# Moving the loads of the output weights in a cross-attention kernel, and dealing the first batch's projection steps anew

## The chip, the core and the metric

The kernel runs on one core of a Trainium2 chip. The metric is device time in microseconds (us), lower is better. The kernel before took 574.34 us, the median of three runs (573.46, 574.34, 575.16). One execution was also profiled; it took 574.06 us, of which 572.2 us are the span between its first and last instruction. All durations below come from that execution, and its times count from the start of the span.

## What is computed

Cross-attention with a layer norm in front and a residual behind, in float32:

```
x   = layernorm(hidden) * gamma + beta          # hidden: 8 x 256 x 1024
Q   = split_heads(x @ Wq.T)                     # 32 heads of 32
K,V = split_heads(ctx), split_heads(ctx)        # ctx: 8 x 256 x 1024
p   = softmax(where(mask, Q K^T / sqrt(32), -inf))
out = hidden + merge_heads(p V) @ Wout.T
```

## The kernel before

The order of instructions is written out by hand: the program calls the engines in the order in which they run, and every engine, SP's DMA queue among them, takes its instructions in that order. A wait of the first in a queue holds all behind it.

**Slots.** The work is cut into 64 slots, one for each of the 8 batches and 8 groups of 4 heads. A loop over n (near line 920) issues slot n as a pipeline. TensorE (PE) makes the scores of group n+1 (`scores`, L479), then the values of group n-2 (`values`, L622), and then whatever matmuls the slot has besides: projections of queries (`make_q`, L340, for the first three batches, `query_product`, L440, later) and steps of the output projection (`product_steps`, L708). VectorE (DVE) and ScalarE (ACT) do the softmax of group n+1 (L515, L519, L526), GpSimd (POOL) multiplies by the reciprocal sums (L528), DVE transposes in 32 x 32 blocks (L534), and ACT sets half of the result aside (L540).

**The copies within the chip.** The transposed probabilities pT have to change partitions before `values` can use them. The tail of each softmax (L595) issues on SP: two copies pT<-pT (L600), then the loads that the slot wants (a list named `between`: keys L136 or values L144, x L130, the residual rows r L150, and in the first eight slots one load of output weights, `load_wo`, L173), and then two copies pT<-pc (L604). The latter overwrite what the former have read, so they wait until those have landed. In slots 0 to 6 the tail is held back and issued in the softmax of the next slot. After it may come pieces of the normalised x on their way to another layout (`move_x`, L327).

**The output projection** of a batch runs during the slots of the next one. It is computed as seven products of half-size blocks (a Strassen-like scheme), each of four steps, so 28 steps for a batch. A step is one 128 x 128 by 128 x 512 product, which the trace shows as two matmuls. The products in their order are A11, A12, S2, S3, A22, S1, S4. Their weights are four blocks of the output weights as loaded (B11, B21, B12, B22; each comes as two loads of 512 KB, `pair` 0 and 1) and four sums of them that POOL forms in the slots 3 to 14 (`sum_wo`, L183: T3 = B22 - B12, T2 = T3 + B11, T4 = B21 - T2, and T1 = B12 - B11 in B12's place).

`steps_of` (L660) says how many of the 28 steps go to which slot of the next batch, and to which of three places in it: 0 is ahead of the slot's values, 1 right behind them, 2 at the slot's end. A plan entry (0, 6, 0) is thus six steps at place 1. For the first batch (b = 0) its own plan holds. Its product A11 goes to a PSUM bank of its own, which ACT copies to SBUF as P1 (`keep_p1`, L716). A12 goes to the one bank of the pool `ps_o`. In slot 10 DVE adds that bank and the residual rows r(0,0) (`store`, L750), after POOL has added P1 to r(0,0) (`add_p1`, L741), and SP sends the sum out. S2 then begins in the same bank, so its first step waits for that store. The next bank reads are `take` (L746) in slots 11 and 12.

**The head**, ahead of the loop, loads the first x, the query weights wq (eight loads of 512 KB, L167), two pairs of keys, one of values and the second x. The weights need no other buffer than their own, so a load of wo waits for no reader. SP has a limited set of DMA semaphores, used in turn, so a DMA also waits for the one that last used its semaphore, some eight DMAs earlier.

**"Traffic of B11"** in the name of the change is the copy of B11's *query* weights to memory and back (`keep_wq`, L400, and `load_ring`, L407). The change leaves it as it is.

Of the kernel before, what the change touches and what calls it, by code (L numbers as in the profile page):

```python
# [59 lines left out]
def xattn_kernel(  # L60
# [16 lines left out]
    NQ = NC  # L77
# [85 lines left out]
    B11, B21, B22, T1, T2, T3, T4 = range(7)  # L163
    B12 = T1

    def load_wq(o):
        nc.sync.dma_start(wq[:, o], wq_[o])  # L167

    def load_wo(which, pair):

        k, h = {B11: (0, 0), B21: (1, 0), B12: (0, 1), B22: (1, 1)}[which]
        rows = woT[ds((NK * k + 2 * pair) * P, 2 * P), ts(h, 512)]
        nc.sync.dma_start(  # L173
            wo[:, which, ts(pair, 2)], rows.rearrange("(c p) q -> p c q", c=2)
        )
# [31 lines left out]
    load_v(0)  # L207
    for o in range(5, 8):
        load_wq(o)


    xnTs, mvs, rstds = {}, {}, {}
# [416 lines left out]
    def copy_at(n):  # L629
# [4 lines left out]
        for r, pv in enumerate(pvs.pop(n)):  # L634
# [20 lines left out]
    STEPS = ((0, 0, 0), (4, 0, 3), (0, 1, 2), (0, 2, 2), (0, 2, 1), (0, 1, 2), (0, 0, 3), (0, 1, 2),  # L655
             (0, 2, 0))
# [3 lines left out]
    def steps_of(b):  # L660
        if b == B - 2:
            return ENDS
        if b == 0:
            return STEPS[:1] + ((0, 6, 0), (0, 2, 2)) + STEPS[3:]
        return STEPS[:1] + ((0, 7, 0),) + STEPS[2:] if b in P1_ASIDE else STEPS

    assert all(sum(map(sum, steps_of(b))) == len(PRODUCTS) * NK for b in range(B - 1))

    def operand(b, name):
# [228 lines left out]
    for b in range(B - 1):  # L898
        done, ends = 0, b == B - 2
        for i, counts in enumerate(steps_of(b)):  # L900
            n = NQ * (b + 1) + i
            for place, k in enumerate(counts):
                steps.setdefault((n, place), []).append((b, range(done, done + k)))
                done += k
        for i, *what in (
            ((2, keep_p1), (3, take_po_q), *((i, copy_po, i) for i in range(3, 8))) if ends else
            ((1, keep_p1), *(((2, add_p1, 0, 0),) if b in P1_ASIDE else ()), (2, store, 0, 0), (3, take, 0, 1), (4, take, 1, 1), (6, store, 1, 0),
             (7, store, 1, 1), (8, store, 0, 1))
        ):
            evacuations[NQ * (b + 1) + i].append((what[0], b, *what[1:]))  # L910
# [6 lines left out]
    for n in range(N):  # L917
        b, i = divmod(n - NQ, NQ)
        new_q = new_qs[n]
        between = []  # L920
# [5 lines left out]
        if n + 3 in firsts or n + 2 in firsts:  # L926
            between, ahead = between + ahead, []
# [4 lines left out]
                between.append(partial(load_res, b, *((0, 0), (0, 1), (1, 1), (1, 0))[i]))  # L932
        between += [partial(load_x, *args) for args in loads[n]]
        between += [partial(load_mask, one) for one in masks[n]]
        if n < NQ:
            which, pair = (
                (B12, 0), (B22, 0), (B11, 0), (B12, 1), (B22, 1), (B11, 1), (B21, 0), (B21, 1)
            )[n]
            between.append(partial(load_wo, which, pair))
        if n == N - 4:  # L940
            again = xp.tile([P, NS, D], F32, tag="x", name="x_again")
            for s in range(NS):
# [192 lines left out]
```

## Time and profile before

| what | value |
|---|---|
| median of three runs | 574.34 us |
| the profiled execution | 574.06 us, span 572.2 us |
| PE busy | 564.6 us, 99% of the span |
| DVE, ACT, POOL busy | 460.2, 411.6, 409.7 us (80, 72, 72%) |
| TensorE clock granted | full in all 40 slices |
| DMA, whole span | 117.98 MB, mean 206 GB/s |
| loads of output weights (wo) | 8 of 512 KB, 5.5 us from issue to landing (median) |
| when they are issued | 34.6, 40.9, 48.3, 57.8, 65.6, 73.2, 82.2 and 86.3 us |

The page of the profile gives shares over the whole span. Here they say only that PE is the engine to watch: at 99% the others matter where they make PE wait. Which waits those are is told by the view of waits, where they are by the timeline, and how busy the DMA engines were at that time by the table of windows (busy time of each engine in a stretch, then the granted clock, the share of the 16 DMA engines and GB/s). In a timeline row the first number is the start, the second the length, and a bracket at the end holds the idle time before and what ended it.

In this execution the scores of slot n start at 22.1 (slot 0), 27.7, 35.1, 42.9, 50.5, 58.1, 65.6, 73.1, 80.7 (slot 8), 88.2, 97.1, 108.0 (slot 11) and 117.2 us, then every 8 to 9.5 us.

### The profile page before, as it was taken

To read this page: it belongs to the slowest core of one execution; us is meant where nothing else is said; L and a number is where in the kernel's file an instruction comes from. 1 tells how busy PE (TensorE), PEld (TensorE's weight loads), DVE (VectorE), ACT (ScalarE), POOL (GpSimd) and SP (SyncE) were. 2 spreads that over 40 slices of the span, in tenths; PEclk is the share of its full clock that TensorE was granted. 3 is DMA by queue.
4 is the path that set the end of the run, shared out by engine and by line. 5 is a ranking of instruction groups with operands and counts; after the bars stand their busy time and mean duration, and the time that the engine had idled before them with its cause. 6 is when DMAs were issued, how large, how long until landed. Compare 5 with 4: busy or idle time off the path is not lost.

```text
span 572.2 us, 20001 instructions
## 1 busy us (share of the span) xinstructions
PE 564.6 (99%) x7162; PEld 392.4 (69%) x7162; DVE 460.2 (80%) x1695; ACT 411.6 (72%) x1425; POOL 409.7 (72%) x677
## 2 busy tenths in 40 slices
PE   8999999999999999999999999999999999999997
PEld 7788885566667677667675677667866767755544
DVE  5897988788868878979898788988888878879823
ACT  4698886777758868688677867778767776769820
POOL 1788898899896896875568576677648657448780
PEclk9999999999999999999999999999999999999999
DMA  8676778766778677887788767896658864536742
GB/s 297 242 193 199 220 230 233 242 183 189 192 240 273 204 190 208 260 219 217 199 240 233 208 184 204 249 274 191 187 147 242 250 201 134 155 97 176 223 148 74
DMA packets 47475, 117.98 MB, mean 206 GB/s; under 512 B 9104, under 2 KB 9872, under 8 KB 47376
## 3 DMA queue, kind: packets, MB, share of 16 engines
q1 hardware_dynamic: 47088, 116.69, 69.5%
q8 instruction: 57, 0.93, 0.7%
q14 instruction: 42, 0.34, 0.2%
q10 hardware_dynamic: 288, 0.01, 0.0%
HBM read 65.28 MB, written 11.53 MB: 134 GB/s over the span
## 4 chain that ended last, share of the span: by engine, by line
PE 86%; DMA 4%; POOL 3%; DVE 3%; ACT 1%; issue 1%; SPq 1%; DVEq 0%; POOLq 0%; ACTq 0%
PE po_S L708 20%; PE pq_A L440 16%; PE sc L479 11%; PE pv L622 11%; PE po_A L708 9%; PE pq L340 9%; PE pq_S L440 6%; PE po_end L775 2%; POOL e L528 2%; DMA wo<-in_woT_dram 2%; DVE e L515 1%; PE po_last L775 1%; DVE pT L534 1%; DMA wq<-in_wq_dram 1%; ACT e L519 1%
## 5 line engine op out<-in xcount | busy, mean ns | idle before, releaser
L528 POOL TENSOR_SCALAR e<-e,rden 128x256 f32<-128x256 f32 x512 | 235.9, 478 | 115.3 <-DVE rden L526 112.6
L519 ACT ACTIVATE e<-e,mn 128x256 f32<-128x256 f32 x512 | 254.0, 501 | 50.5 <-DVE mn L515 49.3
L534 DVE STREAM_TRANSPOSE pT<-e 128x512 f32<-128x512 f32 x256 | 180.9, 707 | 45.0 <-POOL e L528 32.5
L515 DVE CUSTOM_DVE_ANT_0 e<-sc,mb 128x256 f32<-128x256 f32 x512 | 185.5, 416 | 29.0 <-PE sc L479 28.6
L540 ACT COPY pc<-pT 128x512 f32<-128x512 f32 x128 | 79.1, 618 | 68.5 <-DVE pT L534 39.4
L519 ACT ACTIVATION_READ_ACCUMULATOR e<-e,mn 128x1 f32 x512 | 98.1, 192 | 0.0
L340 PE MATMUL pq<-xnT,wq 128*128 128x256 f32 (+1 forms) x368 | 84.1, 383 | 0.0
L340 PEld LDWEIGHTS pq<-xnT,wq 128*128 128x128 f32 x368 | 68.9, 190 | 14.2 <-issue 3.8
L622 PE MATMUL pv<-pT,v 64*32 64x128 f32 x4096 | 74.7, 274 | 0.9 <-DMA pT<-pc 0.9
L479 PEld LDWEIGHTS sc<-k,qa 32*128 32x128 f32 x1024 | 46.2, 184 | 42.3 <-issue 25.2
L708 PE MATMUL po_S<-wo,at 128*128 128x512 f32 x152 | 74.3, 606 | 0.0
L622 PEld LDWEIGHTS pv<-pT,v 64*32 64x32 f32 x4096 | 57.2, 105 | 24.3 <-issue 12.7
L479 PE MATMUL sc<-k,qa 32*128 32x256 f32 x1024 | 73.6, 401 | 0.1
L708 PE MATMUL po_A<-wo,at 128*128 128x512 f32 x128 | 59.5, 606 | 0.0
L708 PE MATMUL po_S<-wo,s 128*128 128x512 f32 x104 | 50.2, 607 | 1.4 <-DVE r L750 1.4
L515 DVE DVE_READ_ACCUMULATOR2_ANT mn<- 128x1 f32 x512 | 42.6, 83 | 0.0
L526 DVE RECIPROCAL rden<-den 128x2 f32<-128x2 f32 x256 | 37.6, 147 | 5.5 <-ACT e L519 4.5
L440 PEld LDWEIGHTS pq_A<-xnT,wq 128*128 128x128 f32 x320 | 37.3, 192 | 4.8 <-issue 4.1
L708 PEld LDWEIGHTS po_A<-wo,at 128*128 128x128 f32 x128 | 23.0, 190 | 25.3 <-issue 23.5
L708 PEld LDWEIGHTS po_S<-wo,at 128*128 128x128 f32 x152 | 25.8, 190 | 19.7 <-issue 19.5
L440 PE MATMUL pq_A<-xnT,wq 128*128 128x128 f32 x320 | 37.3, 275 | 0.0
L741 POOL TENSOR_TENSOR r<-r,p 128x512 f32<-128x512 f32 x23 | 29.4, 1277 | 5.1 <-DMA r<-in_x_dram 5.1
(95 smaller groups left out, 606.5 us busy)
## 6 DMA issues: line engine op xcount, KB each, us to landing
v<-in_kv_dram SPq DMA_DIRECT2D x32, 512.0 KB, 4.5
pT<-pT SPq DMA_DIRECT2D x128, 128.0 KB, 3.1
pT<-pc SPq DMA_DIRECT2D x128, 128.0 KB, 4.4
ring<-kept_T SPq DMA_DIRECT2D x18, 512.0 KB, 5.4
k<-in_kv_dram SPq DMA_DIRECT2D x32, 256.0 KB, 3.9
x<-in_x_dram SPq DMA_DIRECT2D x14, 512.0 KB, 5.7
r<-in_x_dram SPq DMA_DIRECT2D x28, 256.0 KB, 4.8
out_dram<-r SPq DMA_DIRECT2D x28, 256.0 KB, 3.6
```

The costliest lines, as they stand in the source:

```text
L340: nc.tensor.matmul(pqs[n], wq[:, o, c, :], xnTs[b](c), start=(c == 0), stop=(c == NC - 1),)
L440: nc.tensor.matmul(pqs[b][:, o, :], w[:, c], x_[:, c], start=begins and o + c == 0, stop=c == NK - 1, skip_group_check=True,)
L479: nc.tensor.matmul(scs[n][j][:, s, :], qa[r, n % NQ, ts(s, P)], ks[n - n % 2][r, n % 2, :], start=True, stop=True,)
L515: nc.vector.tensor_tensor_reduce(out=e[:, s, :], in0=pss[j][:, s, :], in1=mbs[n // NQ], scale=1.0, scalar=NO_SCORE, op0=ALU.add, op1=ALU.m ...
L519: nc.scalar.activation(e[:, s, :], e[:, s, :], AF.Exp, bias=mn[:, s : s + 1], scale=-1.0, accum_out=den[:, s : s + 1],)
L526: nc.vector.reciprocal(rden, dens[j])
L528: nc.gpsimd.tensor_scalar(es[j][:, s, :], es[j][:, s, :], rden[:, s : s + 1], 1.0, ALU.mult, ALU.mult,)
L534: nc.vector.transpose(pT[:, :, :, j, :, :].rearrange("p a i s k -> p (a i) s k"), es[j].rearrange("p s (b t) -> p b s t", t=K),)
L540: nc.scalar.copy(pc[:, :, ts(j, 2)], pT[:, 1, :, ts(j, 2)])
L622: nc.tensor.matmul(pvs[n][r][j * HD : (j + 1) * HD], vs[n - n % 2][ts(r, 2 * K), i, ds(n % 2 * P + j * HD, HD)], pT[ts(r, 2 * K), :, i, j, ...
L708: nc.tensor.matmul(po, operand(b, name)[:, c], wo[:, which, c], start=begins and c == 0, stop=c == NK - 1, skip_group_check=not begins,)
L741: nc.gpsimd.tensor_tensor(r, r, p1s[b], ALU.add)
```

## The change

Six of the eight wo loads leave the slots and are issued in the head, right behind the last load of query weights: both halves of B12, B22 and B11. The two halves of B21, which stood in slots 6 and 7, move to slots 3 and 4, so that slots 0, 1, 2, 5, 6 and 7 issue no wo load any more. The plan of the first batch changes in its slots 10 to 12: slot 10 gives its two steps at place 2 (the first two of S2) to slot 11, which now runs all four of S2 at place 1 and one of S3 at place 2 (before: two of S2 and two of S3), and slot 12 runs three steps of S3 at place 1 instead of two. After slot 10 eight steps are done instead of ten; after place 1 of slot 11 it is twelve, and at the end of slot 12 seventeen, in both.

```diff
     for o in range(5, 8):
         load_wq(o)
+    for which, pair in ((B12, 0), (B22, 0), (B11, 0), (B12, 1), (B22, 1), (B11, 1)):
+        load_wo(which, pair)
...
         if b == 0:
-            return STEPS[:1] + ((0, 6, 0), (0, 2, 2)) + STEPS[3:]
+            return STEPS[:1] + ((0, 6, 0), (0, 2, 0), (0, 4, 1), (0, 3, 1)) + STEPS[5:]
...
-        if n < NQ:
-            which, pair = (
-                (B12, 0), (B22, 0), (B11, 0), (B12, 1), (B22, 1), (B11, 1), (B21, 0), (B21, 1)
-            )[n]
-            between.append(partial(load_wo, which, pair))
+        if n in (3, 4):
+            between.append(partial(load_wo, B21, n - 3))
```

The plan used elsewhere, `STEPS`, is unchanged; its entries 3 and 4 are (0, 2, 2) and (0, 2, 1).

## The prediction

> **What bounds the kernel now.** I read the waits of TensorE first: between 60 and 545 us it waits for another engine or a transfer twice, and never after 107 us.
>
> ```profile
> PE po_S L708 <- DVE r L750: 1.4, 1, 1.4
> PE pv L622 <- DMA pT<-pc: 0.9, 1, 0.9
> ```
>
> So time is won or lost only where these two waits stand, or where the change makes a new one: a microsecond on PE before 107 us is a microsecond at the end, as long as the others can follow. Next the timeline of PE, which places them (start, length, what ran, idle time before).
>
> ```profile
> 80.67 1.15 PE L479 MATMUL sc<-k,qa 32*128 32x256 f32 x16
> 81.74 1.16 PE L622 MATMUL pv<-pT,v 64*32 64x128 f32 x64
> 82.83 5.45 PE L340 MATMUL pq<-xnT,wq 128*128 128x256 f32 x24
> 88.21 1.15 PE L479 MATMUL sc<-k,qa 32*128 32x256 f32 x16
> 90.22 1.55 PE L622 MATMUL pv<-pT,v 64*32 64x128 f32 x64 [0.86 <-DMA pT<-pc]
> 91.70 5.42 PE L708 MATMUL po_A<-wo,at 128*128 128x512 f32 x12
> ...
> 101.03 3.62 PE L340 MATMUL pq<-xnT,wq 128*128 128x256 f32 x16
> 106.07 1.99 PE L708 MATMUL po_S<-wo,s 128*128 128x512 f32 x4 [1.42 <-DVE r L750]
> 107.99 1.15 PE L479 MATMUL sc<-k,qa 32*128 32x256 f32 x16
> ```
>
> These are slots 8 to 11. Then SP's queue in the timeline, where the loads that move stand:
>
> ```profile
> 82.17 0.43 SPq L173 DMA_DIRECT2D wo<-in_woT_dram  x1
> 82.71 1.15 SPq L604 DMA_DIRECT2D pT<-pc  x2
> 83.95 1.18 SPq L600 DMA_DIRECT2D pT<-pT  x2
> 85.18 0.58 SPq L144 DMA_DIRECT2D v<-in_kv_dram  x1
> 85.81 0.49 SPq L130 DMA_DIRECT2D x<-in_x_dram  x1
> 86.34 0.60 SPq L173 DMA_DIRECT2D wo<-in_woT_dram  x1
> 91.07 1.54 SPq L604 DMA_DIRECT2D pT<-pc  x2
> 92.66 4.96 SPq L327 DMA_DIRECT2D xnT<-xe  x6
> 97.73 1.16 SPq L600 DMA_DIRECT2D pT<-pT  x2
> 98.94 0.59 SPq L136 DMA_DIRECT2D k<-in_kv_dram  x1
> 99.57 1.91 SPq L150 DMA_DIRECT2D r<-in_x_dram  x1
> ```
>
> Both waits come out of this queue. The copies of 82.71 are those that slot 9's values (90.22) read; the DMA view gives 7.3 and 7.4 us to their landing, behind a wo load of 7.2. The r load of 99.57, which lands 4.3 us later, holds the second: POOL's add of P1 starts at 104.02 after 1.17 us idle, DVE's store at 105.33 after 2.77 us idle, and the first S2 step needs the PSUM bank that this store frees.
>
> **The change, part by part.** It adds and removes no arithmetic: eight loads of 512 KB stay eight, 28 steps stay 28, and the other engines keep their order. Three parts count.
>
> *1. The load of slot 6 leaves the queue ahead of slot 9's copies: -1.33 us.* From scores to the next matmuls slot 9 takes 91.70 - 88.21 = 3.49 us, slot 8 82.83 - 80.67 = 2.16; the wait and the stretched pv group cost 1.33. The k load issued at 81.07 lands at 84.1 (3.0 us), the wo load at 89.4; between them an x and the wo load pass, 2.65 us each. Without the latter the copies land at 87.5 to 87.9, and PE wants them at 89.3. The wait goes whole, with 1.4 us to spare. Nothing on PE is late in its place: A11's operands are older.
>
> *2. Slot 7's load goes too, and two S2 steps move behind the next scores and values: -1.59 us.* The q group of 101.03 takes 3.45 us after steps (121.22 to 124.67 in slot 12), so PE was ready at 104.48 and started at 106.07: 1.59. Moved, S2's four steps come 1.08 (scores) and 1.08 (pv) later. With part 1 PE reaches slot 11's scores at 104.48 - 1.33 = 103.15, the values at 104.2, S2 at 105.3. What is late next? The store. SP's copies of 91.07 waited 4.1 us for the copies of 83.95, which took 7.1 us to land; without slot 6's load that is 2.65 less. The moves after them waited 1.2 us for wo loads. So r is issued 3.5 us or more earlier, near 96, and lands near 100; POOL is free at 102.85, its add ends at 104.1, the store at 104.85: half a microsecond before PE wants the bank. If r came no earlier, the store would end at 106.0 and cost PE 0.7 here. The copies for these values (issued 101.58 and 102.1) go near 98 and land by 103.5 (4.5 to 5.4 us), before 104.2. The scores' banks are read out at 102.55.
>
> *3. Six loads in the head: +0.5 us.* 6 x 0.524 = 3.15 MB come behind the last wq load. The windows show these queues full until 22 us and then empty:
>
> ```profile
> 10.00:15.00 5.00, 5.00 (x43) 4.11 (x41) 3.39 (x14) 3.43 (x13) 0.00 (x0) 1.00 1.01 411
> 15.00:20.00 5.00, 4.91 (x28) 4.02 (x28) 4.86 (x19) 3.05 (x12) 2.35 (x4) 1.00 1.03 404
> 24.00:25.00 1.00, 1.00 (x7) 0.86 (x5) 1.00 (x6) 1.00 (x5) 1.00 (x1) 1.00 0.07 20
> ```
>
> (The last columns are the share of the 16 DMA engines and GB/s.) A share of 0.07 is one engine of 16, still at work until nearly 25. At 404 GB/s the loads take 7.8 us: most engines end near 30, that one near 32.7. The first slot's copies (L600, issued 25.40) now queue behind it and land near 33.8 instead of 27.8. SP stands in L604 until then; the second pair follows at 0.6 us distance and lands 2.3 us later: 36.1 and 36.7. PE wants both at 36.15. That is +0.5. The k load, x load and copies that SP issues from 33.5 follow 2 to 3 us late, but no wo load stands among them, and the copies of slot 1 have until 44.0. Bounds: at 404 GB/s with no lag nothing is late, 0. At the 263 GB/s of the window 85 to 90 us, where the DMA share was 1.00 too, the loads take 12.0 us, and PE loses 0.5 + 4.2 = 4.7. I take 0.5: the window 22 to 31 us holds loads from HBM alone, like that from 10 to 20, and no copies within the chip.
>
> The Trainium skill (DMA: Bandwidth & Descriptors, section "Queues, rings and completion order") says that descriptors on one engine are consumed in ring order. It speaks against the change: what is issued after six loads waits for all six. The trace agrees: 2.3 us to landing for the first copies on an empty queue, 7.4 for those behind k, x and wo. The same page's specifications give some 358 GB/s from HBM for a core; by that figure (an estimate) the loads take 8.8 us, 1.0 more, and the sum would be 1.4 instead of 2.4. The measured 404 decides.
>
> The B21 loads in slots 3 and 4 stand where two other loads stood: nothing. POOL's sums of wo tiles waited for no load: nothing. The load issues that leave SP (0.44 us each) stood beside a PE that did not wait, except in slots 6 and 7, counted above.
>
> *What caps it.* After 112 us PE never waits, but its leads are finite. The shortest that I found: POOL forms T1's last quarter at 141.87 to 143.14, and S1's last step reads it at 144.6, 1.45 later. POOL's own chain moves forward by the 1.17 us it idled before the add (it is gapless from 129.5 on, and its gaps before that are waits on DVE, which ran without a wait for PE from 105.33 to 133.9). So 2.6 us pass, not more. The take of slot 11 (113.31, done 113.9) before S3 at 115.4 allows 1.5 + 1.17 = 2.7. From 171 us on POOL idles 4.0 us and is paced by PE again.
>
> **Sum:** -1.33 - 1.59 + 0.5 = -2.4, under the cap of 2.6. The profiled run took 574.06 us (span 572.2), 0.28 below the median of 574.34; the sum gives 571.66 from the one, 571.9 from the other. I say 571.7.
>
> **Rivals.** *A, the wait moves on, or the cap is lower.* In 132 to 140 us POOL is busy 7.95 of 8.00: if r comes no earlier, its chain does not move, T1 caps at 1.45, and the time is 574.06 - 1.45 = 572.6; with slot 11's values late as well (their copies were issued only at 101.58), only part 1 stays: 572.7. For it: that queue has been late since 84 us. Against: two of the loads that made it late are gone. 572.6 to 573.3.
>
> *B, the head costs more, but less than is won by a measurable margin:* copies 2 to 4.5 us late at PE, 573.2 to 575.7.
>
> *C, slower: the queue in the head drains too slowly.* Place: the values of slot 2 at 36.15. Each microsecond by which the second copy pair lands after it is paid in full, as PE has no idle time until 89 us. The gain of 2.9 is gone at 3150/(7.8 + 2.4) = 309 GB/s, and a loss that can be measured begins at 265. At the whole run's mean of 206 GB/s the loads take 15.3 us and the stall is 8.0: 574.06 + 8.0 - 2.9 = 579.2. For it: 263 GB/s at full share did occur. Against: that window is full of on-chip copies.
>
> *D, the change does not do what it says:* the order of instructions shows it does; the head loads stand behind the last wq load on SP, and S2's two steps behind values(9).
>
> **Chances.** A measurement of this kernel tells about 0.3% (1.7 us) from no change. Forecast (571.2 to 572.4): 0.60. A: 0.20. B: 0.10. C: 0.10. A and B are mostly within 0.3%: faster 0.60, same 0.30, slower 0.10. The range takes in the forecast, A and the lower half of B, and at its low end the whole 2.92 with a run's scatter: 570.9 to 574.2. The part-3 bound of 4.7 lies in C's tenth and outside.
>
> **What would show it.** Right: no PE idle time before the values of slot 9 and before S2; r lands before 102; the head's windows from 22 to 30 us at a DMA share near 1; the values of slot 2 start near 36.7. Wrong: values of slot 2 after 38; a new PE wait on copies near 103, on the store near 105, or on POOL near 142; any wait of PE later than that.

## The result, and the profile after

The changed kernel took 572.62 us in the median of 20 runs (571.86 to 574.53), the kernel before 574.37 in 20 runs beside it (573.0 to 576.62): a ratio of 0.9971 [0.996, 0.9982], a gain of 1.75 us where 571.7 us, a gain of 2.4 from the profiled run, had been forecast. The median lies inside the stated range of 570.9 to 574.2, but 0.2 above the 571.2 to 572.4 of the forecast itself. The profiled execution of the change took 571.86 us, span 570.1, and is the quickest of its 20; against the profiled execution of before (574.06) it gains 2.20. What follows reads these two against each other. Two lines were added near the top of the new file, so L481 is L479 of before, L624 is L622, L710 is L708, L752 is L750.

The waits of PE over the whole span of the change (line and what it waited for, us in total, times, longest):

```profile
PE busy L120 <- POOL ring masks.py:199: 1.3, 1, 1.3
PE po_end L777 <- ACT at L637: 0.4, 1, 0.4
PE po_S L710 <- DVE r L752: 0.3, 1, 0.3
```

The first stands in the start-up, the second at the very end. Both waits that the forecast aimed at are gone; a smaller one has come. The timeline of PE in slots 9 to 11 of the change:

```profile
88.20 1.15 PE L481 MATMUL sc<-k,qa 32*128 32x256 f32 x16
89.28 1.16 PE L624 MATMUL pv<-pT,v 64*32 64x128 f32 x64
90.36 5.42 PE L710 MATMUL po_A<-wo,at 128*128 128x512 f32 x12
...
103.24 1.15 PE L481 MATMUL sc<-k,qa 32*128 32x256 f32 x16
104.32 1.16 PE L624 MATMUL pv<-pT,v 64*32 64x128 f32 x64
105.40 3.70 PE L710 MATMUL po_S<-wo,s 128*128 128x512 f32 x8
```

No bracket stands at any of them: slot 9 needs 2.16 us from its scores to its projection steps, as slot 8 did, and S2 starts 1.08 after the values. SP's queue in the same stretch shows why:

```profile
81.60 1.15 SPq L606 DMA_DIRECT2D pT<-pc  x2
...
87.00 1.24 SPq L606 DMA_DIRECT2D pT<-pc  x2
...
94.61 0.45 SPq L150 DMA_DIRECT2D r<-in_x_dram  x1
```

The copies of 81.60 land 4.3 us after issue, where those of 82.71 took 7.4 before. The next pair goes out at 87.00 instead of 91.07, and r at 94.61 instead of 99.57.

How far the change is ahead of before at the start of each slot's scores (before's start less the change's) is the sum so far (slot 62 is the last that makes scores):

| start of slot | 0 to 9 | 10 | 11 | 12 | 13 to 15 | 16 | 17 to 62 |
|---|---|---|---|---|---|---|---|
| ahead, us | 0.0 | 1.3 | 4.75 | 3.5 | 2.7 | 2.1 | 2.1 |

At slot 11, 1.92 us of the 4.75 are the two moved steps (106.07 to 107.99 in before), which leaves 2.83 won. From slot 13 on the same steps are done in both: 0.2 went by then (in slot 11 PE comes to DVE's `take` with no time to spare), 0.5 more in slot 15, and nothing after.

### The profile page after: what moved, and what is told of

The parts are those of the page before. It is cut to its first block, busy times and chain, and to the rows that moved or that the text cites. A ratio compares the mean times of both kernels' runs of the same rounds, so it can differ in the third digit from the quotient of the medians.

```text
span 570.1 us, 19996 instructions
## 1 busy us (share of the span) xinstructions
PE 564.9 (99%) x7162; PEld 392.0 (69%) x7162; DVE 459.4 (81%) x1695; ACT 411.4 (72%) x1425; POOL 410.3 (72%) x677
## 4 chain that ended last, share of the span: by engine, by line
PE 85%; POOL 6%; DVE 4%; issue 2%; ACT 1%; DMA 1%; DVEq 0%; POOLq 0%; ACTq 0%
PE po_S L710 19%; PE pq_A L442 16%; PE sc L481 11%; PE pv L624 10%; PE po_A L710 10%; PE pq L342 8%; PE pq_S L442 6%; POOL e L530 4%; PE po_end L777 2%; DVE e L517 2%; DVE pT L536 1%; PE po_last L777 1%; PE busy L120 1%; POOL wo L183 1%; ACT e L521 1%
## 5 line engine op out<-in xcount | busy, mean ns | idle before, releaser
L481 PEld LDWEIGHTS sc<-k,qa 32*128 32x128 f32 x1024 | 46.1, 184 | 42.0 <-issue 20.5
L710 PE MATMUL po_S<-wo,at 128*128 128x512 f32 x152 | 74.5, 607 | 0.4 <-DVE r L752 0.3
L624 PE MATMUL pv<-pT,v 64*32 64x128 f32 x4096 | 74.4, 274 | 0.0
L481 PE MATMUL sc<-k,qa 32*128 32x256 f32 x1024 | 73.6, 400 | 0.1
L624 PEld LDWEIGHTS pv<-pT,v 64*32 64x32 f32 x4096 | 57.0, 105 | 23.1 <-issue 12.5
L710 PE MATMUL po_A<-wo,at 128*128 128x512 f32 x128 | 59.5, 605 | 0.0
L710 PE MATMUL po_S<-wo,s 128*128 128x512 f32 x104 | 49.9, 605 | 0.0
L710 PEld LDWEIGHTS po_A<-wo,at 128*128 128x128 f32 x128 | 22.9, 189 | 25.4 <-issue 24.5
L710 PEld LDWEIGHTS po_S<-wo,at 128*128 128x128 f32 x152 | 25.6, 190 | 20.8 <-issue 19.3
L637 ACT COPY at<-pv 128x128 f32<-128x128 f32 x128 | 26.2, 253 | 8.7 <-PE pv L624 8.7
```

What stands on the lines that cost most here:

```text
L481: nc.tensor.matmul(scs[n][j][:, s, :], qa[r, n % NQ, ts(s, P)], ks[n - n % 2][r, n % 2, :], start=True, stop=True,)
L624: nc.tensor.matmul(pvs[n][r][j * HD : (j + 1) * HD], vs[n - n % 2][ts(r, 2 * K), i, ds(n % 2 * P + j * HD, HD)], pT[ts(r, 2 * K), :, i, j, ...
L637: nc.scalar.copy(ats[b, k][:, c, :, ts(r, 2), :], pv.rearrange("p a s k -> p s a k"))
L710: nc.tensor.matmul(po, operand(b, name)[:, c], wo[:, which, c], start=begins and c == 0, stop=c == NK - 1, skip_group_check=not begins,)
```

## The experiments

All kernels differ from the changed one by the diff shown; each ratio is to the kernel before, run on the same chip. The medians come from three chips, so across kernels the ratios are to be compared. Leads below are counted from the start of each execution's own slot 0, as the executions start up to 0.65 us apart.

| kernel | median us (runs) | ratio and interval |
|---|---|---|
| loads_only | 574.27 (12) | 0.9995 [0.9978, 1.0013] |
| plan_only | 574.16 (12) | 0.9994 [0.9978, 1.001] |
| redeal | 572.56 (12) | 0.9969 [0.9956, 0.9983] |
| no_head | 575.53 (12) | 1.0023 [1.0008, 1.0039] |
| head_8 | 575.3 (10) | 1.0023 [1.0011, 1.0035] |
| head_10 | 580.03 (4) | 1.0112 [1.0095, 1.0128] |
| one_in_6 | 573.94 (10) | 1.0004 [0.9992, 1.0017] |
| one_in_7 | 573.43 (10) | 0.9984 [0.9972, 0.9996] |
| change_again | 573.47 (12) | 0.9976 [0.9962, 0.9989] |
| x_first | 572.48 (6) | 0.9961 [0.9946, 0.9975] |
| x_first_old_plan | 573.24 (12) | 0.9975 [0.9956, 0.9994] |
| x_first_redeal | 571.92 (6) | 0.9956 [0.9939, 0.9974] |

### Each half alone

**loads_only**: the moved loads with the old plan.

```diff
-            return STEPS[:1] + ((0, 6, 0), (0, 2, 0), (0, 4, 1), (0, 3, 1)) + STEPS[5:]
+            return STEPS[:1] + ((0, 6, 0), (0, 2, 2)) + STEPS[3:]
```

> The loads as in the change, the first batch's steps dealt as before. Theory (two waits removed, each by its own part): the wait for slot 9's copies is gone, but S2 stands in slot 10 again, where PE is ready at 103.1 us and DVE's store ends at 104.5 to 104.6; so PE waits 1.4 us on the store there, and the gain over the kernel before is 106.07 - 104.6 = 1.5 us, 572.9. Rival (the loads alone do it, the new dealing is worth nothing): 572.6, as with the whole change, and no wait on the store.

It gained nothing that can be told (0.9995), against a gain of some 1.5 us expected. One line of the queue of before, and then the timeline of loads_only, from the queue, DVE and PE, say where part 1 went:

```profile
34.07 0.44 SPq L130 DMA_DIRECT2D x<-in_x_dram  x1
```

```profile
36.43 0.45 SPq L130 DMA_DIRECT2D x<-in_x_dram  x1
42.38 0.69 DVE L228 BATCH_NORM_STATS2 st<-x 128x6 f32<-128x512 f32 x1 [2.06 <-DMA x<-in_x_dram]
61.77 5.42 PE L342 MATMUL pq<-xnT,wq 128*128 128x256 f32 x24 [1.25 <-ACT qa L351]
```

The load of the x two batches on, x(2,0), was issued at 34.07 before. Here SP reaches it at 36.43, behind the first slot's copies, which wait for the head's loads. The layer-norm statistics of that x stand in DVE's line in slot 2; DVE waits 2.06 us, the softmax behind it is late, POOL idles 2.37 at 43.83, and PE pays 1.25 in slot 5. The kernel is 1.3 us behind before at slot 6 and level with it at slot 10: part 1 was won and had been lost beforehand. This had not been priced at all, and became the second theory: *the head's price stands on DVE, not at PE's values of slot 2.*

This profiled run, 576.31, is the slowest of its twelve, and loses 2.1 us more in slots 10 and 11. PE waits 1.90 us before S2 where before waits 1.42, and from 0.8 us behind that wait its granted clock is 0.50 for some 3.4 us (estimated from windows of 1 us), so that S2's first two steps take 3.05 us instead of 1.99 and the next scores 1.72 instead of 1.15:

```profile
105.00:110.00 5.00, 3.25 (x8) 1.10 (x12) 3.33 (x8) 2.43 (x8) 5.00 (x11) 0.75 0.86 293
```

(Busy times by engine, then granted clock, DMA share, GB/s; the clock is 0.75 in the mean of these 5 us, 1.00 up to 107 us and 0.50 from 108 to 110.) Three of its twelve runs had a mean clock of 0.997, and they are its slowest; the nine others have a median of 573.85, the 32 of 35 runs of before on that chip with a clock of 0.999 or more 574.37.

**plan_only**: the loads of before with the new plan.

```diff
-    for which, pair in ((B12, 0), (B22, 0), (B11, 0), (B12, 1), (B22, 1), (B11, 1)):
-        load_wo(which, pair)
...
-        if n in (3, 4):
-            between.append(partial(load_wo, B21, n - 3))
+        if n < NQ:
+            which, pair = ((B12, 0), (B22, 0), (B11, 0), (B12, 1),
+                           (B22, 1), (B11, 1), (B21, 0), (B21, 1))[n]
+            between.append(partial(load_wo, which, pair))
```

> The new dealing alone, all eight loads in slots 0 to 7 as before. Theory: the wait for slot 9's copies stays (1.3 us), the copies for slot 11's values land near 106.5 and the r row no earlier than before, so PE waits about 1 us before these values and POOL's chain does not move forward; 0.4 to 1.0 us gained, 573.4 to 574.0. Rival (the dealing alone takes S2's wait off): 1.59 us gained, 572.8.

0.9994, no measurable gain, and a median (574.16) a little above the expected 573.4 to 574.0. It is 0.86 us ahead at slot 13 and 0.30 at slot 16. So the plan alone takes part of the wait before S2, and slot 15 takes most of that back, as it takes 0.5 from the change.

### What caps the gain

**redeal**: slot 11 has S2's four steps and no more, slot 15 one step, and S4's four stand in slot 16.

```diff
-            return STEPS[:1] + ((0, 6, 0), (0, 2, 0), (0, 4, 1), (0, 3, 1)) + STEPS[5:]
+            return STEPS[:1] + ((0, 6, 0), (0, 2, 0), (0, 4, 0), (0, 4, 1), (0, 1, 2), (0, 0, 3), (0, 1, 0), (0, 4, 0))
```

> The change, and in the first batch one step of S3 moved from slot 11 to 12 and two of S4 from slot 15 to 16, so that each comes behind the next scores and values. Theory: the change won 2.84 us up to slot 11 and lost 0.18 on the take of slot 11 and 0.53 on the store of slot 15, which PE now no longer meets: 0.7 us less than with the change, 571.9, profiled span near 569.4, scores of slot 20 and later 2.8 us ahead of the kernel before. Rival (VectorE and GpSimd are the pace there, and the wait comes back at another place, T1's last quarter in slot 15 above all): 572.4 to 572.6, with a new wait of PE on GpSimd near 142 us.

```profile
PE po_S L710 <- POOL wo L183: 0.4, 1, 0.4
```

S4's wait is gone and T1's last quarter on POOL has taken its place, as the rival said; the lead ends at 2.2 us, and 0.9969 cannot be told from the change's 0.9971. Both limits hang on POOL, and the profiled executions together show how closely. In all nine with the change's plan (the change, change_again, plan_only, no_head, head_8, head_10, one_in_6, one_in_7, x_first) S4 starts 0.05 to 0.06 us after the store of slot 15 has ended, and the lead at slot 17 is 0.69 to 0.79 us more than the time by which POOL's add of P1 runs earlier than in before (1.37 in the change, 0.90 in x_first, 0.81 in one_in_7, -0.40 in plan_only). In the two with redeal's plan it is 1.25 and 1.27 more. So the end goes with how early POOL's chain runs, not with what PE has won ahead of it; redeal's plan leaves 0.5 us more room, but in its profiled execution POOL's add came only 0.98 earlier and DVE had waited 0.97 for an x.

### The price of the head

**no_head**: the six loads in slots 0 to 5 as before, B21 doubled into slots 3 and 4, the new plan kept.

```diff
-    for which, pair in ((B12, 0), (B22, 0), (B11, 0), (B12, 1), (B22, 1), (B11, 1)):
-        load_wo(which, pair)
...
+        if n < 6:
+            which, pair = ((B12, 0), (B22, 0), (B11, 0), (B12, 1), (B22, 1), (B11, 1))[n]
+            between.append(partial(load_wo, which, pair))
```

> No load of output weights in the head: six in slots 0 to 5 as before the change, B21's two as a second load in slots 3 and 4; the new dealing. Theory: what counts is that slots 6 and 7 are clear, the head is only a place to put the loads: as with the change, 572.6 within 0.3, the same waits. Rival (the early slots need their queue clear too): SP falls behind in slots 3 to 5, a wait of PE for copies appears between 58 and 90 us, 573.2 or more.

It was slower than before (1.0023). That the head is only a place to put loads, and slots 0 to 5 would do, is refuted for this placement, with two loads each in slots 3 and 4; no other was tried. In its timeline an x is late again, another one, in slot 8, with POOL behind DVE:

```profile
87.95 0.69 DVE L226 BATCH_NORM_STATS2 st<-x 128x6 f32<-128x512 f32 x1 [1.42 <-DMA x<-in_x_dram]
89.39 0.94 POOL L528 TENSOR_SCALAR e<-e,rden 128x256 f32<-128x256 f32 x2 [1.83 <-DVE rden L526]
```

Slot 9 gains 0.4 instead of 1.3 (PE waits 0.8 for ACT's qa there), and less is left of the rest: 0.5 at slot 16. This execution also starts 0.65 us later than before's and drops back once by 0.7 near slot 43. Whether those two belong to the kernel or to the execution one profile can't tell, so the size of the loss in the median stays open.

**head_8** and **head_10**: all eight loads in the head; and ten, where B12 and B22's first halves are loaded twice, so that the transfer alone grows.

```diff
-    for which, pair in ((B12, 0), (B22, 0), (B11, 0), (B12, 1), (B22, 1), (B11, 1)):
+    for which, pair in ((B12, 0), (B22, 0), (B11, 0), (B12, 1), (B22, 1), (B11, 1), (B21, 0), (B21, 1)):
...
-        if n in (3, 4):
-            between.append(partial(load_wo, B21, n - 3))
```

(head_10 has `, (B12, 0), (B22, 0)` more.)

> All eight loads in the head, none in the slots. Theory (queue drained in ring order at some 388 GB/s): the two more loads take 2.7 us; the first slot's copies land near 35.0 instead of 32.4, the second pair is issued then and lands at 37.3 and 37.9, and PE, which wants them at 36.1, waits 1.8 us before the values of slot 2. The small waits near 112 and 146 us shrink in turn, as PE comes later: 1.0 us more than the change, 573.6. Rival (the head has more room than that, or the copies pass the loads): no wait, 572.6.

> Ten loads in the head: the eight, and B12's and B22's first halves once more into the same place. Theory: each microsecond of queue beyond the room is paid in full: 2.7 us more than with eight loads, PE waits 4.5 us before the values of slot 2, 576.1 to 576.5, slower than the kernel before. Rival (softer, PE's other work or the later waits take most of it up): 574 or less.

The waits of PE in the window 20 to 60 us, of head_8 and then of head_10:

```profile
PE pv L624 <- DMA pT<-pc: 2.5, 2, 2.3
```

```profile
PE pv L624 <- DMA pT<-pc: 4.6, 1, 4.6
```

The second pair of first copies goes out at 32.40 us in the change, 36.33 in head_8, 38.56 in head_10; PE's longest wait at the values of slot 2 is 0, 2.3 and 4.6. Rival C's mechanism is real and stands where it was placed. Two loads take 2.6 us at 404 GB/s; the ninth and tenth make the wait 2.3 us longer. In head_8 PE starts these values 2.4 us after the pair goes out; by that the six loads leave 1.3 us of room in the change's execution (an estimate), and none in x_first_redeal's below.

Both medians lie above what was expected (573.6, and 576.1 to 576.5), because the wait is not the whole price. From the scores of slot 2 to those of slot 3 head_8 loses 4.3 us and head_10 7.4. About the end of the wait PE's granted clock falls to 0.50, for some 3.4 us in head_8 (40.5 to 44) and 6.8 in head_10 (39.7 to 46.5). The 24 query matmuls behind the values take 7.17 us in head_8 and 7.00 in head_10, where the change takes 5.49. Here is head_8's row, and the granted clock of head_10 in 40 slices of its span, in tenths:

```profile
40.38 7.17 PE L342 MATMUL pq<-xnT,wq 128*128 128x257 f32 x24
```

```profile
PEclk9988999999999999999999999999999999999999
```

In head_10 the values themselves take 2.58 us instead of 1.47. So 1.7 us of the 4.3, and 2.6 of the 7.4, fall in the stretch of the slower clock; the rest is the wait. DVE's wait for x(2,0) is there too (2.33 in head_8), but PE is late by then and does not wait for it. head_8's runs with a clock of 0.999 or more (six of ten) have a median of 574.85; all four of head_10 lie at 0.994 to 0.996.

### Which of the two late loads mattered

**one_in_6** and **one_in_7**: B21's second half back in slot 6, or in slot 7.

```diff
-        if n in (3, 4):
-            between.append(partial(load_wo, B21, n - 3))
+        if n in (3, 6):
+            between.append(partial(load_wo, B21, n // 6))
```

(one_in_7 has 7 for 6.)

> The change, but B21's second half is loaded in slot 6, ahead of the copies for slot 9's values. Theory: the wait of 0.9 us and the stretched values of slot 9 (1.33 us in all) come back, and the r row lands later, so POOL's chain moves forward less: 573.3 to 574.0. Rival (one load less on the queue is enough, since slots 0 to 5 are clear): 572.6.

> The change, but B21's second half is loaded in slot 7, behind the copies for slot 9's values. Theory: no wait in slot 9; the r row and the copies of slot 9's tail come 1 to 2 us later than with the change but still in time, or the store ends up to 0.5 us after PE wants its bank: 572.6 to 573.2.

With the load in slot 6 the wait of part 1 is back:

```profile
90.39 1.63 PE L624 MATMUL pv<-pT,v 64*32 64x128 f32 x64 [0.68 <-DMA pT<-pc]
```

The lead at slot 10 is 0.1 us, and the gain is gone (1.0004). With the load in slot 7 the lead at slot 10 is 1.3, at slot 13 2.1, and at slot 17 1.6 (0.9984; 573.43 us, slightly above the expected 572.6 to 573.2). So the load of slot 6 carries part 1 by itself. What that of slot 7 is worth is not shown: one_in_7 ends 0.5 us behind the change because POOL's add runs 0.56 later, but the add does not wait for r there. DVE had waited 0.34 us for another x in slot 8 (at 86.47), issued ahead of that load; x_first, which has no load in slot 7, waits 0.31 at the same place and ends with the same 1.6.

### The second theory: an x that comes late on DVE

**change_again** is the changed kernel beside the next three. **x_first** loads x(2,0) in the head ahead of five wo loads, and B11's second half in slot 0 in its place; **x_first_old_plan** and **x_first_redeal** are the same with the old plan and with redeal's.

```diff
-    for which, pair in ((B12, 0), (B22, 0), (B11, 0), (B12, 1), (B22, 1), (B11, 1)):
-        load_wo(which, pair)
...
+    load_x(2, 0)
+    for which, pair in ((B12, 0), (B22, 0), (B11, 0), (B12, 1), (B22, 1)):
+        load_wo(which, pair)
...
-        between += [partial(load_x, *args) for args in loads[n]]
+        between += [partial(load_x, *args) for args in loads[n] if args != (2, 0)]
+        if n == 0:
+            between.append(partial(load_wo, B11, 1))
```

> The changed kernel itself, beside the three below on one chip. Theory (new): its six loads in the head make the load of the third batch's x late, on which VectorE's statistics in slot 2 stand in line; five of the six other profiles with these loads show VectorE waiting 0.6 to 2.1 us there, the one profile of the change none. So a second profile of it shows a wait of 0.5 to 1.5 us before these statistics, PE's lead in slots 11 to 17 smaller by it, and about 572.6. Rival: the profile with no wait is the usual one.

> The change with two loads swapped: the first half of the third batch's x goes into the head ahead of the wo loads, and B11's second half into its place in slot 0. Theory (new): VectorE never waits for x in slot 2, GpSimd's chain is never late, so the usual time is that of the change's best runs: 571.9 to 572.2, 0.5 us less than the change beside it. Rival (the head's loads cost nothing, the scatter is from elsewhere): 572.6, as the change.

> The same swap, with the first batch's steps dealt as before the change. Theory: with the dealing as before, every lateness of VectorE and GpSimd passes through the store to S2 in slot 10, which is why the loads alone gave nothing; with x in time the store ends at 104.6 and the gain of 1.3 to 1.5 us comes: 573.0. Rival (the loads alone give nothing for another reason): 574.3.

> The same swap with the steps of S3 and S4 moved as in the run redeal. Theory: 0.3 to 0.4 us below the run with the swap alone, 571.5 to 571.8, with one wait of 0.4 us on T1's last quarter in slot 15 left. Rival (all of it is taken back by that wait): as the swap alone.

What the profiled executions show of x(2,0):

| kernel | issue, us | from slot 0's scores, us | DVE's wait for it, us | lost on PE by slot 6, us |
|---|---|---|---|---|
| before | 34.07 | 11.99 | 0 | 0 |
| the change | 35.55 | 13.50 | 0 | 0 |
| change_again | 35.92 | 13.78 | 0.45 | 0 |
| one_in_6 | 36.28 | 13.85 | 0.63 | 0 |
| one_in_7 | 36.14 | 13.91 | 0.82 | 0 |
| redeal | 36.01 | 14.06 | 0.97 | 0.2 |
| loads_only | 36.43 | 14.14 | 2.06 | 1.3 |
| x_first and x_first_old_plan | in the head | | 0 | 0 |

Counted from each execution's own slot 0, DVE's wait grows with the lateness of the issue, and in slot 5 PE pays only for what goes beyond some 0.8 us. (x_first_redeal does not wait for it either, but lost 0.4 at the values of slot 2.) The expectation of change_again, a wait of 0.5 to 1.5 us and 572.6, was missed by little in the wait and by more in the time: 573.47, on a chip where the kernel before took 575.07.

The clearest pair is the old plan's. loads_only lost 1.3 us by slot 6; x_first_old_plan loses nothing there, is 1.3 ahead at slot 10 and 1.3 ahead at slot 62. Its only wait of PE between 20 and 545 us is the one that the plan was to remove:

```profile
PE po_S L708 <- DVE r L750: 1.4, 1, 1.4
```

In the medians all three plans are quicker with x first: 0.9995 against 0.9975, 0.9976 against 0.9961, 0.9969 against 0.9956. Only the middle pair ran on the same chip, and each pair's intervals overlap. In that pair all six runs of x_first took 571.9 to 573.0 us, and eleven of the twelve of change_again 573.15 to 575.15. The profiles alone do not show this gain for the new plan: change_again's profiled run (572.12) is its quickest, with little of the fault in it, and x_first's (572.76) starts 0.4 us later and keeps a lead of 1.7 us against 1.9, and DVE waits 0.31 us in it for the x of slot 8. So for the new plan the second theory is not shown: DVE can be held by another late x, which stands behind no load of the head, and at slot 17 the lead of change_again, with its wait of 0.45, is only 0.1 smaller than the change's.

x_first_redeal has the lowest median here, 571.92 (571.5 to 571.8 had been expected), and beats the kernel before; against the change the intervals overlap. Its profiled run, the slowest of its six (573.78), waits 1.94 us for x in slot 8, as no_head does, and 0.25 for copies at the values of slot 2: neither place has much to spare.

## Why the prediction was right, and where it was not

**Part 1, -1.33: right.** The copies landed by 86.5, earlier than the 87.5 to 87.9 worked out. 1.3 us at slot 10 in the change, in one_in_7 and in x_first_old_plan; 0.1 with the load back in slot 6.

**Part 2, -1.59: right in sum.** 2.83 - 1.33 = 1.50 by slot 11. r was issued at 94.61, not near 96, and landed in 2.9 us, at 97.5 instead of the predicted 100. What is late next was named rightly in kind: of POOL's add and DVE's store the store ends last, and before PE wants the bank at 105.40 (first two rows of the last fence of this section). The two halves need each other: x_first_old_plan keeps the wait of 1.4 before S2, plan_only gains 0.86.

**Part 3, +0.5 at the values of slot 2: mis-sized and misplaced.** The window 24 to 26 us of the change (busy times by engine, then granted clock, DMA share, GB/s):

```profile
24.00:26.00 2.00, 2.00 (x11) 1.75 (x10) 2.00 (x11) 2.00 (x8) 2.00 (x1) 1.00 1.05 388
```

The head's loads ran at 385 to 399 GB/s from 20 to 28 us, near the 404 taken. The Trainium skill (DMA: Bandwidth & Descriptors, section "Specifications") has some 358 GB/s from HBM for a core; the four windows of 2 us from 20 to 28 us lie above it. SP issued the second pair of copies at 32.40, not near 33.8, so PE paid nothing: the values of slot 2 start at 36.12, before at 36.15. In x_first_redeal the pair went out at 33.86 and PE waited 0.25; the predicted stall is thus there in a late execution. What the working had called "2 to 3 us late, but no wo load stands among them" was the sentence that failed: the x load among them has a reader on DVE, and the runs with six loads in the head show 0 to 2.06 us of waiting there, of which PE paid up to 1.3. Rival C's "paid in full" was too low: beyond six loads PE pays the wait and the slower clock after it.

**The cap of 2.6: mis-sized.** "The shortest that I found" was not the shortest. T1 was read rightly: its last quarter ends at 140.51 + 1.28 = 141.79, and S1's last step starts at 141.89. But the store of slot 15 was overlooked. In before it ends at 148.14 and S4 begins at 148.97, a slack of 0.83:

```profile
147.49 0.65 DVE L750 TENSOR_TENSOR r<-po_S,r 128x512 f32<-128x512 f32 x1
148.97 1.88 PE L708 MATMUL po_S<-wo,at 128*128 128x512 f32 x4
```

In the change:

```profile
102.62 1.28 POOL L743 TENSOR_TENSOR r<-r,p 128x512 f32<-128x512 f32 x1
103.93 0.69 DVE L752 TENSOR_TENSOR r<-po_A,r 128x512 f32<-128x512 f32 x1 [1.55 <-POOL r L743]
137.78 0.71 DVE L536 STREAM_TRANSPOSE pT<-e 128x512 f32<-128x512 f32 x1 [1.67 <-POOL e L530]
140.51 1.28 POOL L183 TENSOR_TENSOR wo<-wo 128x512 f32<-128x512 f32 x1
146.02 0.65 DVE L752 TENSOR_TENSOR r<-po_S,r 128x512 f32<-128x512 f32 x1
146.73 1.98 PE L710 MATMUL po_S<-wo,at 128*128 128x512 f32 x4 [0.26 <-DVE r L752]
```

POOL's sum moved from 141.87 to 140.51, by 1.36 (1.17 had been predicted), while PE was 2.67 ahead; DVE now waits 1.67 us for POOL, and the store moved by 1.47. 0.83 + 1.47 = 2.3 can pass; 2.1 did. That is the wait "later than that" which the prediction listed as a sign of being wrong, and rival A's mechanism with a smaller price.

**Sum.** 2.83 of the predicted 2.92 were won, the head cost nothing instead of 0.5, and 0.7 was lost in slots 11 and 15 where nothing had been deducted. The forecast of -2.4 against -2.2 in the profile is near because the two errors nearly cancel, which is luck. The 0.45 us from the profile's gain to the median's are not settled: late x loads on DVE may have a part in it, since change_again waits for one and the change does not, but that wait took only 0.1 us of the lead, and both executions are the quickest of their kernels.

**Rivals.** The median, 572.62, lies at the edge of what A was given (572.6 to 573.3), and a lower cap was part of it; its other part, r no earlier, did not come. B and C did not decide at six loads; C's wait comes from eight. D was out.

## What to carry to other kernels

When a burst of loads is put ahead of a queue, follow every transfer behind it to its reader, on every engine that works in order: a prefetch whose reader is two batches of data away in the program may stand only a few microseconds ahead of it on DVE. When a gain is capped by slacks, list each hand-over between engines up to the point where the leads are large again, and move each by what its own engine gains, not by what PE gains. Where a new wait of the busiest engine is priced, look at its granted clock after the wait as well. And when a profiled execution is the quickest of its kernel, trust it for the places and the median for the size.

## What had not been expected of the hardware

**A long wait cost more than its length.** The three profiled executions in which PE waited 1.9 us or more at one place between 20 and 545 us (loads_only 1.90, head_8 2.28, head_10 4.63) are the three with a mean granted clock below 1.000. In each the clock fell to 0.50 between 1.2 us ahead of the end of that wait and 1.8 behind it, for some 3.4 us in the first two and 6.8 in the third. After the waits of up to 1.42 us in the eleven other executions it did not fall. Of 83 runs of before beside the experiments nine have a mean clock below 0.999 and took 575.5 to 579.0 us; of 32 of the change none has. That before's wait of 1.4 us sometimes grows to such a length would fit, but no profile caught it.

**The end of the burst scatters.** The first copies behind the head's six loads were over at times that differed from run to run: the pair that waits for them went out between 32.40 and 33.86 us in kernels whose heads carry the same bytes, six wo loads or five and an x. The start of slot 0 accounts for less than 0.4 us of that.

**A small copy waits for the loads ahead of it.** The same 128 KB copy took 2.2 to 2.4 us on an empty queue, 4.3 behind a k and an x load, 7.4 with a wo load more.
